# A gated cross-attention and expert layer: the last two chunks turned by row tiles, the upper rows' choice of experts in front of the lower rows, and side work of the first slots moved

## The chip, the cores and the metric

The kernel runs on one core of a Trainium2 chip. The metric is the device time of one execution in microseconds, lower is better. The core's engines each work through a queue of their own in order: TensorE (PE: matmuls; PEld: its weight loads), VectorE (DVE), ScalarE (ACT), GpSimd (POOL), and SyncE (SP), which here only issues transfers. They wait for one another through semaphores.

## The reference

The input `x` has 8 batches of 512 rows and 2048 columns, in float32. First a windowed cross-attention is added to it, then a mixture of expert biases:

```python
def _layernorm(x, axis=-1, eps=1e-05): ...
# attention, in windows of 128 columns; 8 heads of 32; W* are 256 x 512, Wo is 512 x 256
q = Wq @ patches(layernorm(x)) + bq;  k = Wk @ patches(layernorm(x)) + bk;  v = Wv @ patches(ctx) + bv
attn = softmax(where(mask > 0, q^T k / sqrt(32), -1e9))
o = gelu(attn @ v, exact);  out = (Wo @ o + bo) * mask
x = x + tanh(g_xattn) * out
# experts: each of the 8 x 512 rows (2048 long) chooses 8 of 64
flat = layernorm(x)
scores = softmax(flat @ router_weight^T + router_bias)
topk_w, topk_idx = top_k(scores, 8);  w_dense = topk_w scattered to 64 places
out = flat * topk_w.sum() + w_dense @ expert_bias
x = x + tanh(g_ffn) * out
```

The choice of experts needs a whole row: the row's mean and variance and its 64 logits are sums over all 2048 columns.

## The kernel before

**Tiles.** A batch is cut into four chunks of 512 columns (`NCH = 4`), 32 chunks in all. A chunk is a tile of 128 partitions by four row tiles `m = 0..3` (128 rows each) by 512 columns. Each chunk is two slots `g` of 256 columns, that is of two windows. The main loop runs over the slots `g = 0..61`; the last chunk `z` and what hangs on it is written out behind the loop. The order of all instructions is written by hand (`manual_schedule`): each engine gets its instructions in the order in which the Python code names them, and no planner moves them.

**A slot of the loop.** `scores(g)` makes the heads' scores; `weigh` and `weighed` multiply the weights of slot `g - 2` with the values and copy the result; `maxima` (VectorE) adds the mask and finds each row's maximum, `exps` (ScalarE) takes exponentials and sums, `divide` (a reciprocal on VectorE and a product on GpSimd) normalises, `turn` and `turned` transpose the weights on TensorE and copy them out on ScalarE. `queries_and_keys` makes the queries and keys of the next chunk by a seven-product scheme (L356), whose partial sums go through VectorE (L363 to L383) and GpSimd (L370, L377); the lines L363 and L364, a copy and an add on VectorE, must be done before its fifth block may start. `read_x` takes statistics of later batches (`bn_stats` on VectorE, L245) from pieces called `raw`, and after each piece SP issues the load of the next one. `weight_sums_in_place` (L197) and the scaling of the output bias (L791) run once, ahead of slot 0.

**Behind a chunk.** `gelu` on ScalarE; `attend(ch, m)` multiplies by the output weights (`po`, L524), adds bias and mask on VectorE (L530) and adds the result to the chunk's rows in `xr` on GpSimd or VectorE (L533); `statistics2` takes `bn_stats` of them (L543). `turn_x(ch, k)` transposes 128 columns of all four row tiles (`px`, L548), so it needs all four to be complete. `logits` (`pl`, L559) multiplies the four transposed tiles with the router's weights and `logits_out` (L577) adds them up over the chunks.

**The choice of experts of a batch.** `aggregate` turns statistics into mean and reciprocal deviation (VectorE L228, then seven short GpSimd instructions L230 to L236); `gather` (`pg`, L592) transposes the logits back to rows, `choose` (L622, L625) scales them and takes the maximum, `choose_exps` (ScalarE, L631), `select` (VectorE L646 to L656, GpSimd L657 to L660) finds the top eight and the row's factor and offset, and `turn_weights` (`pw`, L671, and a copy on ScalarE, L675) gives the matrix `wT`. With it part `k = 2 * j + mp` of the batch, chunk `j` and row tiles `2 * mp` and `2 * mp + 1`, is finished: `scale_x` (L687 on GpSimd, L685 on ScalarE) scales the rows, `mixed` (`pb`, L698) multiplies the chosen weights with the experts' biases, and one of three adds the two: `added` on VectorE (L716); `with_x` and `taken_out`, an identity matmul into the same bank (L723) and a copy on ScalarE (L730); or `copied`, a copy on ScalarE and an add on GpSimd (L739, L741). Then `stored` (L707) sends 512 KB to the output, on SP's queue unless another is named.

**The end.** In the last batch `b` the choice is made twice, for the upper row tiles 0 and 1 (`up`) and for the lower ones 2 and 3 (`low`), so that the even parts of the batch may go out while the lower rows are still being made. The chunk `z` is already turned by row tiles (`turn_last`, lines L1105 to L1109), the chunk `z - 1` by columns. Mixed in are the parts 5, 6 and 7 of the batch before. Matmul results behind the loop share six banks in turn (`late`), transposes two banks (`ps_tr`).

Of the kernel before, what the change touches and what calls it, by code (L numbers as in the profile page):

```python
# [9 lines left out]
F32 = mybir.dt.float32  # L10
AF = mybir.ActivationFunctionType
ALU = mybir.AluOpType
# [10 lines left out]
def flamingo_gated_kernel(  # L23
# [170 lines left out]
        nc.vector.tensor_tensor(ws4, w12, ws2, ALU.subtract)  # L194

    def weight_sums_in_place():
        nc.vector.tensor_tensor(w21, w11, w21, ALU.subtract)  # L197
        nc.scalar.activation(w22, w22, AF.Copy, scale=-1.0)

    half = const.tile([P, NM], F32, name="half")  # L200
# [503 lines left out]
    def stored(b, k, queue, i0, i1):  # L704
        j, mp = k // 2, k % 2
        ch, ms = b * NCH + j, slice(2 * mp + i0, 2 * mp + i1)
        queue.dma_start(rows_of(out, b, columns(ch))[:, ms, :], xr[ch][:, ms, :])  # L707
        if ms.stop == NM:
            del xr[ch]
# [25 lines left out]
    def copied(b, k, i):  # L735

        j, mp = k // 2, k % 2
        t = work.tile([P, CW], F32, tag="raw", name=f"mixed_{b}_{k}_{i}", bufs=2)
        nc.scalar.copy(t, held[b, k][i])  # L739
        xc = xr[b * NCH + j][:, 2 * mp + i, :]  # L740
        nc.gpsimd.tensor_tensor(xc, t, xc, ALU.add)  # L741
        if i == 1:
            del held[b, k]
            stored(b, k, nc.sync, 0, 2)

    def mix(b, k):
        mixed(b, k)
        added(b, k)
# [39 lines left out]
    load_later_weights()  # L788

    nc.scalar.activation(tgates, gates, AF.Tanh)  # L790
    nc.vector.tensor_scalar_mul(bo_sb, bo_sb, tgates[:, 0:1])  # L791
    NPIECE = NM * S // SW
    queue = [(b, i) for b in range(1, B) for i in range(NPIECE)]
    for i in range(2):
# [19 lines left out]
    for g in range(NG - NH):  # L814
# [21 lines left out]
        def turn_(k):  # L836
            if g1 is not None:
                turn(g1, k)
                turned(g1, k)
# [24 lines left out]
        def read_x(n, pieces=pieces):  # L864

            for b, i in pieces[:n]:
                stats_x(b, i)
                if queue:
                    load_raw(*queue.pop(0))
            del pieces[:n]  # L870

        exps(g, 0)
        if even:
            if xch is not None:
                for m in (2, 3):
                    attend(xch, m)
                del os_[xch], mks[xch]
            exps(g, 1)
            exps(g, 2)
            if g > 0:  # L880
                mask(nxt)
            read_x(len(over), over)
            turn_(0)
            turn_(1)
            exps(g, 3)
            if fin != 4:
                for k in steps:
                    scale_x(mb, k)
            if g > 0:
                divide(g, 0)  # L890
            if g == 0:
                load_mask(2)
        else:
            exps(g, 1)
            if lch is not None:
                logits(lch)
                logits_out(lch)
            read_x(len(over), over)
            turn_(0)
            exps(g, 2)  # L900
            exps(g, 3)
            for k in steps:
                scale_x(mb, k)
            if g > 1:
                divide(g, 0)
            b1 = g // SPB + 1
            if g % SPB == 5 and b1 < B:
                ln1[b1] = aggregate(st1.pop(b1), S // 512, f"1_{b1}")
                shares_of_mean(b1)


        def between(i):
            if even:
                if g == 0 and i == 0:
                    divide(g, 0)
                    mask(nxt)
                turn_x_(i)
            elif i == 0:
                if g == 1:
                    divide(g, 0)  # L920
                turn_(1)
                if fin == 3:
                    gather_halves(b4)
                if pch is not None:
                    gelu(pch)
            else:
                turn_(2)
                if pch is not None and nxt < last:
                    load_mask(nxt + 1)
# [19 lines left out]
        def stats():  # L949

            sch = xch if fin != 4 else None
            if fin == 5:
                sch = ch - 2
            if sch is not None:
                for m in range(NM):
                    statistics2(sch, m)
            read_x(PER)

        if fin != 4:
            stats()  # L960
# [120 lines left out]
    mix(b - 1, 4)  # L1081

    late += [0, 1, 2, 3, None, None]
    for m in (0, 1):
        attend(z - 1, m, tag=t_raw)
    turn_(g, 2, 3)
    for m in range(NM):
# [2 lines left out]
    weigh(g)  # L1090
    weighed(g)
    gelu(z)

    table_of_exps()
    attend(z - 1, 3, tag=t_raw)
    scale_x(b - 1, 5)
    for m in (0, 1):
        statistics2(z - 1, m)


    xz = work.tile([P, KC, NM, P], F32, tag="xn", name="xz")
    for k in range(KC):
        x1T[z, k] = xz[:, k, :, :]

    def turn_last(m):  # L1105
        px = ps_tr.tile([P, KC, P], F32, tag="tr", name=f"px_{z}_m{m}")
        for k in range(KC):
            nc.tensor.transpose(px[:, k, :], xr[z][:, m, k * P : (k + 1) * P], ident)
        nc.scalar.copy(xz[:, :, m, :], px)  # L1109

    def rows_known(ms):
        nmean, rs = aggregate(st2[b], NCH, f"2_{b}", ms[0], ms[-1] + 1)
        experts.setdefault(b, {}).update(nmean=nmean, rs=rs)

    up, low = range(NM // 2), range(NM // 2, NM)
    attend(z, 0, engine=nc.vector, tag=t_raw)
    statistics2(z, 0)
    turn_x(z - 1, 0)
    attend(z, 1, engine=nc.vector, tag=t_raw)
    statistics2(z, 1)  # L1120
    rows_known(up)
    scale_x(b - 1, 6)
    turn_x(z - 1, 1)
    mixed(b - 1, 5)
    for k in range(2, KC):
        turn_x(z - 1, k)
    for m in low:
        statistics2(z - 1, m)
    added(b - 1, 5)
    turn_last(0)  # L1130
    turn_last(1)
    logits(z - 1)
    logits_out(z - 1)
    logits(z, slice(0, NM // 2))
    logits_out(z, slice(0, NM // 2))
    mixed(b - 1, 6, stop=False)
    gather(b, up)
    choose(b, up)
    choose_exps(b, up)
    scale_x(b - 1, 7)  # L1140
    attend(z, 2, engine=nc.vector, tag=t_raw)
    statistics2(z, 2)
    with_x(b - 1, 6, 0)
    taken_out(b - 1, 6, 0)
    attend(z, 3, engine=nc.vector, tag=t_raw)
    statistics2(z, 3)
    rows_known(low)
    select(b, up)
    turn_last(2)
    with_x(b - 1, 6, 1)  # L1150
    taken_out(b - 1, 6, 1)
    turn_last(3)
    mixed(b - 1, 7)
    logits(z, slice(NM // 2, NM))
    logits_out(z, slice(NM // 2, NM))
    turn_weights(b, (0,))
    gather(b, low)
    choose(b, low)
    choose_exps(b, low)
    added(b - 1, 7)  # L1160

    scale_x(b, 0)
    scale_x(b, 2, range(2), nc.scalar)
    scale_x(b, 4)
    mixed(b, 0, stop=False)
    for i in range(2):
        with_x(b, 0, i)
        taken_out(b, 0, i)
    mixed(b, 2)
    select(b, low)  # L1170
    turn_weights(b, (1,))
    added(b, 2)
    scale_x(b, 6, range(2), nc.scalar)
    mix(b, 4)
    scale_x(b, 1)
# [5 lines left out]
    for i in range(2):  # L1181
        copied(b, 3, i)
        scale_x(b, 7, (i,), nc.scalar)
    mix(b, 5)
    mixed(b, 7)
    added(b, 7, (nc.sync, nc.scalar))
# [33 lines left out]
```

## Time and profile before

| | |
|---|---|
| median of three runs | 1313.66 us (1313.34 to 1313.7) |
| the profiled execution | 1313.84 us |
| its span in the profile | 1311.7 us |
| TensorE busy | 1294.1 us, 99% |
| VectorE, ScalarE, GpSimd busy | 923.1, 875.6 and 795.4 us |
| moved by transfers | 173.40 MB, mean 132 GB/s |

The span is the time from the first to the last event of the profile; the execution's own time has about 2.1 us more around it. A busy TensorE is one with a matmul in flight. In rows of the timeline the first number is the start in us from the span's start, the second the duration, and a bracket at the end gives the idle time of that engine just before the row and what ended it. In the chain of waits TensorE has 92% of the span; VectorE has 3%, ScalarE 2%.

### The profile page before, as it was taken

The numbers are of one execution on the slowest core, as the hardware profiler recorded it, in microseconds if no ns is written. First come the engines' busy times: TensorE is split into PE (matmuls) and PEld (weight loads), VectorE is DVE, ScalarE is ACT, GpSimd is POOL, SyncE is SP. The second block draws the span as 40 slices with busy tenths as digits, with TensorE's granted clock in tenths as the row PEclk, the third lists the DMA queues.
The fourth block names the chain that finished last, engine by engine and source line by source line (L and its number), as shares of the span: only waits on it lengthen the run. The fifth ranks groups of instructions, "written<-read, shape, count | busy, mean of one in ns | idle before, by whom it ended". The sixth has DMA issues, their size and how long they took to land.

```text
span 1311.7 us, 27799 instructions
## 1 busy us (share of the span) xinstructions
PE 1294.1 (99%) x9544; PEld 944.4 (72%) x9544; DVE 923.1 (70%) x3607; ACT 875.6 (67%) x2843; POOL 795.4 (61%) x815
## 2 busy tenths in 40 slices
PE   8999999999999999999999999999999999999997
PEld 6777777777777777777777777777777777777653
DVE  4777667677677767777677776677776776666776
ACT  2776776676675776856676766677756767657654
POOL 3655556775566755576655666656666665566644
PEclk9999999999999999999999999999999999999999
DMA  8344424253344452454443453433544413423224
GB/s 288 95 122 112 112 92 137 99 168 112 131 153 150 134 168 92 138 168 134 148 138 105 153 169 122 161 106 125 165 150 132 161 62 125 138 100 101 74 73 176
DMA packets 109693, 173.40 MB, mean 132 GB/s; under 512 B 9200, under 2 KB 43632, under 8 KB 109424
## 3 DMA queue, kind: packets, MB, share of 16 engines
q1 hardware_dynamic: 107776, 169.27, 40.0%
q10 hardware_dynamic: 1776, 2.36, 0.5%
q8 instruction: 75, 1.23, 0.4%
q14 instruction: 66, 0.54, 0.2%
HBM read 138.06 MB, written 33.55 MB: 131 GB/s over the span
## 4 chain that ended last, share of the span: by engine, by line
PE 92%; DVE 3%; ACT 2%; DMA 1%; issue 0%; POOL 0%; SPq 0%; DVEq 0%; ACTq 0%
PE qk L356 27%; PE po L524 17%; PE pv L393 15%; PE pt L472 8%; PE sc L418 5%; PE pa L494 5%; PE pb L698 5%; PE pl L559 4%; PE px L548 4%; ACT at L449 1%; PE pf L323 1%; DVE st L543 1%; DMA cx<-in_ctx 1%; DVE at L437 0%; DVE st L245 0%
## 5 line engine op out<-in xcount | busy, mean ns | idle before, releaser
L458 POOL TENSOR_TENSOR at<-at,rsum 128x1024 f32<-128x1024 f32 x128 | 244.1, 1907 | 291.4 <-DVE rsum L457 274.3
L449 ACT ACTIVATE at<-at,nmx 128x128 f32<-128x128 f32 x1024 | 399.1, 396 | 3.0 <-DVE nmx L437 3.0
L393 PE MATMUL pv<-wv_sb,cx 128*128 128x256 f32 x1024 | 238.5, 381 | 2.4 <-DMA cx<-in_ctx 2.4
L524 PE MATMUL po<-o,wo_sb 128*128 128x512 f32 x512 | 234.1, 599 | 0.4 <-ACT o L518 0.4
L437 DVE CUSTOM_DVE_ANT_0 at<-sc,m 128x128 f32<-128x128 f32 x1024 | 220.8, 287 | 7.8 <-PE sc L418 7.8
L393 PEld LDWEIGHTS pv<-wv_sb,cx 128*128 128x128 f32 x1024 | 188.4, 191 | 25.0 <-DMA cx<-in_ctx 2.8
L533 POOL TENSOR_TENSOR xr<-t,xr 128x512 f32<-128x512 f32 x124 | 161.4, 1314 | 65.9 <-DVE t L530 65.9
L449 ACT ACTIVATION_READ_ACCUMULATOR at<-at,nmx 128x1 f32 x1024 | 198.8, 194 | 0.0
L476 ACT COPY o<-pa 128x512 f32<-128x512 f32 x63 | 37.0, 587 | 229.0 <-PE pa L494 229.0
L476 ACT COPY atT<-pt 128x512 f32<-128x512 f32 x254 | 141.2, 579 | 52.8 <-PE pt L472 52.6
L524 PEld LDWEIGHTS po<-o,wo_sb 128*128 128x128 f32 x512 | 94.3, 190 | 100.6 <-issue 83.9
L472 PEld LDWEIGHTS pt<-ident,at 128*128 128x128 f32 x1024 | 121.7, 141 | 56.7 <-issue 35.3
L472 PE MATMUL pt<-ident,at 128*128 128x128 f32 x1024 | 150.6, 275 | 0.7 <-ACT atT L476 0.3
L530 DVE SCALAR_TENSOR_TENSOR t<-po,bo_sb,mk 128x512 f32<-128x512 f32 x128 | 95.9, 749 | 62.9 <-PE po L524 62.9
L476 ACT COPY x1T<-px 128x512 f32<-128x512 f32 x120 | 70.4, 587 | 95.6 <-PE px L548 95.5
L356 PE MATMUL qk<-xt,wq_sb 128*128 128x256 f32 x496 | 128.0, 381 | 2.0 <-DVE u L364 2.0
L356 PE MATMUL qk<-xn,wk_sb 128*128 128x256 f32 x496 | 127.5, 380 | 0.0
L356 PE MATMUL qk<-xn,ws 128*128 128x256 f32 x496 | 127.3, 379 | 0.0
L356 PEld LDWEIGHTS qk<-xn,ws 128*128 128x128 f32 x496 | 94.2, 190 | 12.8
L716 DVE TENSOR_TENSOR xr<-pb,xr 128x512 f32<-128x512 f32 x122 | 78.2, 686 | 29.4 <-PE pb L698 29.4
L356 PEld LDWEIGHTS qk<-xn,wk_sb 128*128 128x128 f32 x496 | 89.4, 190 | 9.7
L418 PEld LDWEIGHTS sc<-ks,qs 32*128 32x128 f32 x2048 | 63.2, 186 | 45.3 <-DVE t L530 18.2
(123 smaller groups left out, 2081.9 us busy)
## 6 DMA issues: line engine op xcount, KB each, us to landing
out_dram<-xr SPq DMA_DIRECT2D x63, 512.0 KB, 3.5
cx<-in_ctx SPq DMA_DIRECT2D x62, 512.0 KB, 5.3
raw<-in_x SPq DMA_DIRECT2D x112, 256.0 KB, 3.4
xn<-in_x SPq DMA_DIRECT2D x28, 1024.0 KB, 7.7
xr<-in_x SPq DMA_DIRECT2D x28, 1024.0 KB, 7.6
mk<-in_mask_Bx1x_ff SPq DMA_DIRECT2D x32, 256.0 KB, 5.1
xr<-in_x SPq DMA_DIRECT2D x12, 256.0 KB, 6.3
cx<-in_ctx ACTq DMA_DIRECT2D x2, 512.0 KB, 6.5
```

The source lines that it names most:

```text
L356: nc.tensor.matmul(out_, w_[:, j, es], xb[:, j, :], start=(j == 0), stop=(j == NM // 2 - 1))
L393: nc.tensor.matmul(pv[:, i, :], cx[:, m, i * W : (i + 1) * W], wv_sb[:, m, :], start=(m == 0), stop=(m == NM - 1),)
L418: nc.tensor.matmul(sc[r][:, i, e, :], qss[ch][rows[r], e, ws], kss[ch][rows[r], e, ws], start=True, stop=True,)
L437: nc.vector.tensor_tensor_reduce(p["at"][i][:, e * HR + r, :], p["sc"][r][:, i, e, :], bias, -1.0, BIG, ALU.add, ALU.min, p["nmx"][:, r, i ...
L449: nc.scalar.activation(at, at, AF.Exp, bias=p["nmx"][:, r, i, e : e + 1], scale=-1.0, accum_out=p["rsum"][:, i, h : h + 1],)
L458: (engine or nc.gpsimd).tensor_tensor(p["at"][i], p["at"][i], rs[:, :, None].to_broadcast([P, H, W]), ALU.mult)
L472: nc.tensor.transpose(pt[:, r, :], p["at"][i][:, e * HR + r, :], ident)
L476: (engine.tensor_copy if engine is nc.vector else engine.copy)(out_, in_)
L524: nc.tensor.matmul(po[:, cs], wo_sb[:, e, m * P : (m + 1) * P], os_[ch][:, e, cs], start=(e == 0), stop=(e == NE - 1),)
L530: nc.vector.scalar_tensor_tensor(t[:, cs], po[:, cs], bo_sb[:, m : m + 1], mks[ch][:, cs], ALU.add, ALU.mult)
L533: (engine or nc.gpsimd).tensor_tensor(xc, t[:, cs], xc, ALU.add)
L716: nc.vector.tensor_tensor(xc, pt, xc, ALU.add)
```

## The change

In the first slots, the subtract of `weight_sums_in_place` and the scaling of `bo_sb` go from VectorE to GpSimd. `read_x` is left out at the end of slot 0, and slot 1 takes those two pieces in the middle of `queries_and_keys` instead of behind the logits.

At the end, both chunks `z - 1` and `z` are turned by row tiles (`turn_row`). In front stands what the choice of the upper rows needs: the upper rows of both chunks, their logits, `gather`, `choose` and `choose_exps`. The lower rows of `z - 1` and `z` follow, with `select` and `turn_weights` of the upper rows among them, and the lower rows' choice is made among the first finished parts of the last batch. The store of part 3 is named behind that of part 5.

```diff
@@ -194,7 +194,7 @@
         nc.vector.tensor_tensor(ws4, w12, ws2, ALU.subtract)
 
     def weight_sums_in_place():
-        nc.vector.tensor_tensor(w21, w11, w21, ALU.subtract)
+        nc.gpsimd.tensor_tensor(w21, w11, w21, ALU.subtract)
         nc.scalar.activation(w22, w22, AF.Copy, scale=-1.0)
 
     half = const.tile([P, NM], F32, name="half")
@@ -741,7 +741,6 @@
         nc.gpsimd.tensor_tensor(xc, t, xc, ALU.add)
         if i == 1:
             del held[b, k]
-            stored(b, k, nc.sync, 0, 2)
 
     def mix(b, k):
         mixed(b, k)
@@ -788,7 +787,7 @@
     load_later_weights()
 
     nc.scalar.activation(tgates, gates, AF.Tanh)
-    nc.vector.tensor_scalar_mul(bo_sb, bo_sb, tgates[:, 0:1])
+    nc.gpsimd.tensor_scalar_mul(bo_sb, bo_sb, tgates[:, 0:1])
     NPIECE = NM * S // SW
     queue = [(b, i) for b in range(1, B) for i in range(NPIECE)]
     for i in range(2):
@@ -895,7 +894,8 @@
             if lch is not None:
                 logits(lch)
                 logits_out(lch)
-            read_x(len(over), over)
+            if g > 1:
+                read_x(len(over), over)
             turn_(0)
             exps(g, 2)
             exps(g, 3)
@@ -924,6 +924,8 @@
                 if pch is not None:
                     gelu(pch)
             else:
+                if g == 1:
+                    read_x(len(over), over)
                 turn_(2)
                 if pch is not None and nxt < last:
                     load_mask(nxt + 1)
@@ -954,7 +956,9 @@
             if sch is not None:
                 for m in range(NM):
                     statistics2(sch, m)
-            read_x(PER)
+
+            if g > 0:
+                read_x(PER)
 
         if fin != 4:
             stats()
@@ -1081,7 +1085,30 @@
     mix(b - 1, 4)
 
     late += [0, 1, 2, 3, None, None]
-    for m in (0, 1):
+
+
+    up, low = range(NM // 2), range(NM // 2, NM)
+    rows_ = {}
+    for ch in (z - 1, z):
+        rows_[ch] = rows = work.tile([P, KC, NM, P], F32, tag="xn", name=f"rows_{ch}")
+        for k in range(KC):
+            x1T[ch, k] = rows[:, k, :, :]
+
+    def turn_row(ch, m):
+        px = ps_tr.tile([P, KC, P], F32, tag="tr", name=f"px_{ch}_m{m}")
+        for k in range(KC):
+            nc.tensor.transpose(px[:, k, :], xr[ch][:, m, k * P : (k + 1) * P], ident)
+        nc.scalar.copy(rows_[ch][:, :, m, :], px)
+
+    def rows_known(ms):
+        nmean, rs = aggregate(st2[b], NCH, f"2_{b}", ms[0], ms[-1] + 1)
+        experts.setdefault(b, {}).update(nmean=nmean, rs=rs)
+
+    def last_rows(m):
+        attend(z, m, engine=nc.vector, tag=t_raw)
+        statistics2(z, m)
+
+    for m in up:
         attend(z - 1, m, tag=t_raw)
     turn_(g, 2, 3)
     for m in range(NM):
@@ -1090,86 +1117,67 @@
     weigh(g)
     weighed(g)
     gelu(z)
-
     table_of_exps()
-    attend(z - 1, 3, tag=t_raw)
+    for m in up:
+        statistics2(z - 1, m)
     scale_x(b - 1, 5)
-    for m in (0, 1):
-        statistics2(z - 1, m)
-
-
-    xz = work.tile([P, KC, NM, P], F32, tag="xn", name="xz")
-    for k in range(KC):
-        x1T[z, k] = xz[:, k, :, :]
-
-    def turn_last(m):
-        px = ps_tr.tile([P, KC, P], F32, tag="tr", name=f"px_{z}_m{m}")
-        for k in range(KC):
-            nc.tensor.transpose(px[:, k, :], xr[z][:, m, k * P : (k + 1) * P], ident)
-        nc.scalar.copy(xz[:, :, m, :], px)
-
-    def rows_known(ms):
-        nmean, rs = aggregate(st2[b], NCH, f"2_{b}", ms[0], ms[-1] + 1)
-        experts.setdefault(b, {}).update(nmean=nmean, rs=rs)
-
-    up, low = range(NM // 2), range(NM // 2, NM)
-    attend(z, 0, engine=nc.vector, tag=t_raw)
-    statistics2(z, 0)
-    turn_x(z - 1, 0)
-    attend(z, 1, engine=nc.vector, tag=t_raw)
-    statistics2(z, 1)
+    for m in up:
+        turn_row(z - 1, m)
+    for m in up:
+        last_rows(m)
     rows_known(up)
     scale_x(b - 1, 6)
-    turn_x(z - 1, 1)
+    ups, lows = slice(0, NM // 2), slice(NM // 2, NM)
+    logits(z - 1, ups)
+    logits_out(z - 1, ups)
+    for m in up:
+        turn_row(z, m)
+    attend(z - 1, 3, tag=t_raw)
+    logits(z, ups)
+    logits_out(z, ups)
     mixed(b - 1, 5)
-    for k in range(2, KC):
-        turn_x(z - 1, k)
-    for m in low:
-        statistics2(z - 1, m)
-    added(b - 1, 5)
-    turn_last(0)
-    turn_last(1)
-    logits(z - 1)
-    logits_out(z - 1)
-    logits(z, slice(0, NM // 2))
-    logits_out(z, slice(0, NM // 2))
-    mixed(b - 1, 6, stop=False)
     gather(b, up)
     choose(b, up)
     choose_exps(b, up)
     scale_x(b - 1, 7)
-    attend(z, 2, engine=nc.vector, tag=t_raw)
-    statistics2(z, 2)
+    added(b - 1, 5)
+    statistics2(z - 1, 2)
+    mixed(b - 1, 6, stop=False)
+    last_rows(2)
     with_x(b - 1, 6, 0)
     taken_out(b - 1, 6, 0)
-    attend(z, 3, engine=nc.vector, tag=t_raw)
-    statistics2(z, 3)
+    select(b, up)
+    scale_x(b, 0)
+    for m in low:
+        turn_row(z - 1, m)
+    turn_weights(b, (0,))
+    statistics2(z - 1, 3)
+    last_rows(3)
     rows_known(low)
-    select(b, up)
-    turn_last(2)
     with_x(b - 1, 6, 1)
     taken_out(b - 1, 6, 1)
-    turn_last(3)
+    logits(z - 1, lows)
+    logits_out(z - 1, lows)
+    turn_row(z, 2)
     mixed(b - 1, 7)
-    logits(z, slice(NM // 2, NM))
-    logits_out(z, slice(NM // 2, NM))
-    turn_weights(b, (0,))
+    turn_row(z, 3)
+    added(b - 1, 7)
+
+    scale_x(b, 2, range(2), nc.scalar)
+    mixed(b, 0, stop=False)
+    logits(z, lows)
+    logits_out(z, lows)
+    with_x(b, 0, 0)
+    taken_out(b, 0, 0)
     gather(b, low)
+    with_x(b, 0, 1)
+    taken_out(b, 0, 1)
+    scale_x(b, 4)
     choose(b, low)
     choose_exps(b, low)
-    added(b - 1, 7)
-
-    scale_x(b, 0)
-    scale_x(b, 2, range(2), nc.scalar)
-    scale_x(b, 4)
-    mixed(b, 0, stop=False)
-    for i in range(2):
-        with_x(b, 0, i)
-        taken_out(b, 0, i)
-    mixed(b, 2)
+    mix(b, 2)
     select(b, low)
     turn_weights(b, (1,))
-    added(b, 2)
     scale_x(b, 6, range(2), nc.scalar)
     mix(b, 4)
     scale_x(b, 1)
@@ -1182,6 +1190,7 @@
         copied(b, 3, i)
         scale_x(b, 7, (i,), nc.scalar)
     mix(b, 5)
+    stored(b, 3, nc.sync, 0, 2)
     mixed(b, 7)
     added(b, 7, (nc.sync, nc.scalar))
 # ---- launch: one core; inputs and outputs as the reference has them ----
```

## The prediction

> **What bounds the kernel now.** I read the page first: its first line of busy times, then the chain.
>
> ```profile
> PE 1294.1 (99%) x9544; PEld 944.4 (72%) x9544; DVE 923.1 (70%) x3607; ACT 875.6 (67%) x2843; POOL 795.4 (61%) x815
> ```
>
> TensorE is busy for all but 17.6 us of the 1311.7 us span, so time can only come from its idle places or from the tail behind its last matmul. The stretches by 25 us show 25.00 of 25 between about 225 and 1225 us; what is idle lies in the first 125 us and in the last 87. The list of who waited for whom gives the early part, TensorE's rows:
>
> ```profile
> PE qk L356 <- DVE u L364: 2.0, 3, 1.1
> ```
>
> Three waits for VectorE in `queries_and_keys`: 0.56 us at 41.1, 1.09 at 50.6, 0.35 at 79.5. The first two are slots 0 and 1. For the end I read each engine's timeline from 1245 us; TensorE's rows first, then VectorE's (start, us, ..., idle before):
>
> ```profile
> 1282.74 0.66 PE L592 MATMUL pg<-ident,lgT 128*128 128x64 f32 x4
> ...
> 1292.00 0.33 PE L671 MATMUL pw<-ident,rest 128*128 128x128 f32 x1
> 1292.57 0.66 PE L592 MATMUL pg<-ident,lgT 128*128 128x64 f32 x4 [0.24 <-DVE lgT L577]
> 1293.16 1.13 PE L698 MATMUL pb<-eb_sb,wT 64*128 64x512 f32 x4
> 1294.89 1.99 PE L723 MATMUL pb<-xr,ident 128*128 128x512 f32 x4 [0.59 <-POOL xr L687]
> 1296.80 1.13 PE L698 MATMUL pb<-eb_sb,wT 64*128 64x512 f32 x4
> 1297.86 0.33 PE L671 MATMUL pw<-ident,rest 128*128 128x128 f32 x1
> 1298.12 6.07 PE L698 MATMUL pb<-eb_sb,wT 64*128 64x512 f32 x24
> ```
>
> ```profile
> 1290.21 0.11 DVE L646 RECIPROCAL es<-es 128x2 f32<-128x2 f32 x1
> ...
> 1291.65 0.29 DVE L656 TENSOR_TENSOR rest<-lg,rest 128x128 f32<-128x128 f32 x1
> ...
> 1298.03 7.38 DVE L716 TENSOR_TENSOR xr<-pb,xr 128x512 f32<-128x512 f32 x12 [0.77 <-PE pb L698]
> ```
>
> `pg` opens a choice of experts, `pw` closes it. For the upper rows 9.3 us lie between, for the lower rows 5.3 us, and TensorE has other matmuls there; neither `pw` makes it wait long. The last add ends at 1305.41. What follows is transfers (stretches: PE, PEld, DVE, ACT, POOL, clock, DMA share, GB/s):
>
> ```profile
> 1302.00:1304.00 2.00, 2.00 (x8) 0.76 (x6) 2.00 (x4) 2.00 (x4) 1.48 (x2) 1.00 1.00 375
> ...
> 1306.00:1308.00 2.00, 0.00 (x0) 0.00 (x0) 0.00 (x0) 0.00 (x0) 0.00 (x0) 0.53 1.02 378
> 1308.00:1310.00 2.00, 0.00 (x0) 0.00 (x0) 0.00 (x0) 0.00 (x0) 0.00 (x0) 0.50 1.03 383
> 1310.00:1312.00 2.00, 0.00 (x0) 0.00 (x0) 0.00 (x0) 0.00 (x0) 0.00 (x0) 0.50 0.06 21
> ```
>
> The last batch stores 8 x 512 KB. At 380 GB/s that is 1.38 us each, 11.0 in all; they run from 1298.4 to 1310.1 almost without a gap. So the end is set by when stores can start and by holes between them, and only then by the last add.
>
> **The start.** Leaving VectorE ahead of slot 0's `maxima`: the subtract of L197 (0.60 from start to start) and the product of L791 (0.13), less 0.1 for the mask bias to land: `maxima` starts at 36.17, not 36.79, and with it L363 and L364, so the wait of 0.56 at 41.1 goes, 0.6 us. On GpSimd the two cost 1.27 (row L282, same shape) and 0.29 (row L658); its queue is free from 35.76 to 41.85, and the subtract's reader, the fifth block of L356, comes at 40.5. Nothing.
> Two `bn_stats` leave slot 0 (45.20 to 46.35, 1.15 us), so slot 1's `maxima` can start 1.75 earlier and the wait of 1.09 goes too. But ScalarE is late next: behind the exponentials of slot 0 it runs four norms (2.92 us), starts slot 1's exponentials at 45.65 in place of 46.66, and the fourth transpose of slot 0's weights needs its copy: at 52.9, not 53.96. So 1.05 us stay of 1.7. The `bn_stats` reappear between L378 and L382, where VectorE idles 0.43: `qs` then comes 0.2 late with 3 us to its reader. SP takes the `cx` load past two `raw` loads; those are issued about 7 us later and land near 55 to 56 (3.5 us each), where VectorE waits about 1 us for them, ahead of `vT` at 57.1: cover is 0.9 us. After this TensorE is full, so I carry **-1.05** to the end; bounds -0.4 (slow landing) and -1.7 (no wait for ScalarE).
>
> **The end.** I laid every instruction from 1265.6 us on end to end in each engine's order, with the rows' durations: `po` 1.78 a pair, four transposes 0.45, half `pl` 0.92, `pb` 0.53, `L723` 0.86, mask-and-bias 0.75, add 0.70, `bn_stats` 0.62, copy 0.49, GpSimd add 1.27, scale 0.76, statistics chain 2.3, selection 1.75 to `rest`, restart after a wait 0.12. Laid so, the order of before gives its last add at 1305.1 (trace 1305.4) and TensorE waits of 2.1 us. The new order:
> 1. `po` of the last chunk waits for `gelu`: ScalarE ends it at 1270.3. Before, `po` of row 3 (1.78) covered that; now only two `turn_row` (0.9): wait 1.1. Second `turn_row(z,1)` waits 0.8 for VectorE's add.
> 2. `pg` of the upper rows starts at 1280.5, not 1282.4: 1.9 earlier, since 2.8 us of lower-row work is behind it.
> 3. Next come `pb` 6, `po(z,2)` (ends 1284.0), L723, two `turn_row`, done at 1285.6, then `pw`. But on VectorE the selection is queued behind `po(z,2)`'s three instructions (t, add, stats: 1284.0 to 1286.2), and ends at 1288.0. Wait **2.5**, and everything behind `pw` is held: `po(z,3)`, the lower logits.
> 4. So the lower rows' `pg` slips from 1292.3 to 1296.8. Behind it only L723 (0.86) and `pb` 2 (1.06) stand before the lower `pw`; the chain is `choose` and maximum 0.85, exponentials at 1298.8 (behind the second `taken_out` on ScalarE), two adds of part 2 (to 1300.1), selection to 1301.9. Wait **2.8**.
> TensorE waits 7.1 against 2.1; fewer restarts give back 0.3: its last matmul and the last add come 4.6 us later, at 1309.8. GpSimd's add of row 3 of `z-1` goes behind the statistics chain and a scale, ending at 1282.3 with its reader at 1285.1: free. Its scale of part 4 goes behind the lower rows' statistics chain, ending at 1296.8 for an add at 1303: free. On SP the stores of the batch before shift by +3.3, +2.5 and -0.6 us; none of their buffers is wanted again. Stores: part 0 is issued at 1298.9 (1297.2), part 2 at 1300.2, but part 4 only at 1304.4 (1299.7): a hole of 2.7 us in the transfers. Six stores remain, 8.3 us from 1305.7: last transfer ends 1314.0 against 1310.2. Part 3's store behind part 5's lets part 5 out without waiting for GpSimd; in before that wait cost one 0.3 us hole. The end: **+3.8**; bounds +2.7 (the shortest landing, 2.7 us, after the last issue) and +4.6.
>
> **The clock, row against rule.** The trace has one earlier long wait of TensorE:
>
> ```profile
> 12.30 8.86 PE L393 MATMUL pv<-wv_sb,cx 128*128 128x256 f32 x32 [2.36 <-DMA cx<-in_ctx]
> ```
>
> ```profile
> 12.50:13.00 0.50, 0.50 (x2) 0.41 (x2) 0.06 (x1) 0.00 (x0) 0.34 (x2) 0.50 1.02 358
> ...
> 15.50:16.00 0.50, 0.50 (x3) 0.41 (x2) 0.28 (x2) 0.00 (x0) 0.10 (x1) 0.63 1.12 350
> 16.00:16.50 0.50, 0.50 (x4) 0.42 (x4) 0.00 (x0) 0.00 (x0) 0.42 (x2) 1.00 1.10 348
> ```
>
> After 2.36 us of waiting the granted clock was 0.50 from 12.5 to 15.8: 3.3 us at half speed, 1.7 us lost. After the last matmul (1304.2) it fell at 1306.05, 1.9 us on. Waits of 1.1 us and less left it at 1.00. The Trainium skill, "TensorE: Matmul & The Clock Gate", section "What's actually happening", says the gate closes after a whole idle window of about 3.4 us, in windows that run free of the kernel. By the page neither 2.5 nor 2.8 us closes it, and the sum is -1.05 + 3.8 = +2.75, 1316.4. By the row each can, if it fills over half of a window, which its place decides. An estimate: at 1.9 us filled of 3.4 (3.3 by the row), (3.4 + 2.5 - 2 x 1.9) / 3.4 = 0.6 for the first wait, 0.7 for the second. Each drop costs 1.7 us (0 if it misses; TensorE has no other slack between the two `pw`, and in the last stretch the twelve `pb` set the pace at half clock). I side with the row and count one drop: **+1.7**.
> Sum: -1.05 + 3.8 + 1.7 = +4.45 on the profiled execution's 1313.84 (span 1311.7 and 2.1 around it), which stands 0.18 over the median of 1313.66. From the median: 1318.1.
>
> **Rivals.**
> Both waits close the gate: 1319.8. For: both exceed 2.36. Against: windows may split a wait.
> None does: 1316.4. For: the page. Against: the rows above.
> The start brings nothing, its stalls turning into waits for the late `raw` loads: 1319.1. Against: 0.9 us of cover before `vT`.
> The other side: the earlier upper choice is covered. If VectorE's selection is done when TensorE reaches each `pw`, both waits (5.2 with restarts 5.5) are absent: the last add comes at 1304.3, part 0's store is out at 1296.4, and 8 stores without a hole end 11.0 us after 1297.7, at 1308.7, 1.5 earlier than before; with the start 1311.1, on the edge of 0.2% faster. For: `pg` does come 1.9 earlier. Against: VectorE keeps its order, and the selection stands behind `po(z,2)`. It turns where the two waits together are under 2.5 us.
>
> **How the numbers follow.** One drop 0.38, both 0.28, none 0.16 (by the estimate above, tilted a little to the page), no gain at the start 0.08, covered 0.10. A measurement of this kernel tells about 0.2%, 2.6 us: faster ends at 1311.0, slower begins at 1316.3. "None" lies on the upper limit and "covered" on the lower; half of the one and four tenths of the other fall within. Faster 0.06, same 0.12, slower 0.82. Range 1315.4 to 1320.6: the first four cases, with about 1 us of bounds at either end.
>
> **What would show it.** Right: `pw` L671's two rows with idle of 2 to 3 us before them, released by VectorE's `rest`; lower `pg` at 1295 or later (less the start's 1 us); clock under 1.00 in a stretch after one; a hole in the transfers between parts 2 and 4; the wait of L356 for L364 under 1 us. Wrong: `pw` without idle, or last add before 1307 with the clock at 1.00.

## The result and the profile after

| | before | after |
|---|---|---|
| median | 1313.54 us | 1320.12 us (four runs, 1319.06 to 1320.96) |
| ratio of the times | | 1.0049, 95% interval 1.0038 to 1.0061 |
| the profiled execution | 1313.84 us | 1319.98 us |
| its span | 1311.7 us | 1317.9 us |

The change makes the kernel 6.6 us slower. The prediction said 1318.1 us, with a range of 1315.4 to 1320.6 and 0.82 for slower. The direction and the mechanism are those predicted; the size is near that of its first rival, 1319.8, in which both waits lower the clock.

The page's line of busy times, and TensorE's rows in the list of who waited for whom (us in total, times, longest):

```profile
PE 1294.7 (98%) x9552; PEld 943.3 (72%) x9552; DVE 922.5 (70%) x3606; ACT 872.1 (66%) x2843; POOL 796.3 (60%) x817
```

```profile
PE pw L671 <- DVE rest L656: 5.5, 2, 3.2
...
PE po L524 <- ACT o L518: 1.1, 2, 0.8
...
PE qk L356 <- DVE u L364: 1.0, 2, 0.7
```

The busy times are those of before within a few us. What is new is the first row: TensorE stands still for 5.5 us in two waits for the selection of the experts. The last row is the start: two waits and 1.0 us, where before had three and 2.0.

TensorE's timeline at the end (start, duration, in brackets the idle time before):

```profile
1279.15 0.66 PE L592 MATMUL pg<-ident,lgT 128*128 128x64 f32 x4
...
1286.87 0.30 PE L671 MATMUL pw<-ident,rest 128*128 128x128 f32 x1 [2.36 <-DVE rest L656]
1287.00 3.33 PE L524 MATMUL po<-o,wo_sb 128*128 128x512 f32 x4
...
1297.65 0.55 PE L592 MATMUL pg<-ident,lgT 128*128 128x64 f32 x4
...
1299.05 1.13 PE L698 MATMUL pb<-eb_sb,wT 64*128 64x512 f32 x4
1303.33 0.33 PE L671 MATMUL pw<-ident,rest 128*128 128x128 f32 x1 [3.15 <-DVE rest L656]
1303.59 7.12 PE L698 MATMUL pb<-eb_sb,wT 64*128 64x512 f32 x24
```

The upper rows' `pg` and `pw` come 3.6 and 5.1 us earlier than before, the `pw` after a wait; the lower rows' `pg` and `pw` come 5.1 and 5.5 us later. The four matmuls of `po` behind the first wait (row tile 3) take 3.33 us, where those of row tile 2 took 1.98 at 1280.79; the last 24 `pb` take 7.12 in place of 6.07.

VectorE's timeline shows what the two `pw` wait for:

```profile
1282.82 0.75 DVE L530 SCALAR_TENSOR_TENSOR t<-po,bo_sb,mk 128x512 f32<-128x512 f32 x1 [0.31 <-PE po L524]
1283.60 0.69 DVE L533 TENSOR_TENSOR xr<-t,xr 128x512 f32<-128x512 f32 x1
1284.33 0.69 DVE L543 BATCH_NORM_STATS2 st<-xr 128x6 f32<-128x512 f32 x1
1284.94 0.15 DVE L646 RECIPROCAL es<-es 128x2 f32<-128x2 f32 x1
...
1286.43 0.29 DVE L656 TENSOR_TENSOR rest<-lg,rest 128x128 f32<-128x128 f32 x1
...
1300.28 1.29 DVE L716 TENSOR_TENSOR xr<-pb,xr 128x512 f32<-128x512 f32 x2 [1.17 <-PE pb L698]
1301.49 0.15 DVE L646 RECIPROCAL es<-es 128x2 f32<-128x2 f32 x1
...
1302.98 0.29 DVE L656 TENSOR_TENSOR rest<-lg,rest 128x128 f32<-128x128 f32 x1
```

In each case the selection (L646 to L656, 1.8 us) begins in the very moment in which a group named ahead of it ends: the mask-and-bias, add and statistics of `last_rows(2)` for the upper rows, the two adds of part 2 for the lower rows. The exponentials that it needs had ended on ScalarE at 1281.5 and 1300.4, 3.4 and 1.1 us before. So the upper wait is a matter of VectorE's queue alone. Of the lower wait's 3.15 us the two adds explain 1.1; the rest is the time that the choice itself takes, with too few matmuls named beside it.

The stretches of time (us, busy of PE, PEld, DVE, ACT, POOL, then TensorE's granted clock, DMA share, GB/s) show what the waits do besides:

```profile
1287.00:1288.00 1.00, 1.00 (x3) 0.53 (x3) 0.32 (x1) 0.37 (x1) 0.81 (x3) 0.65 0.00 0
...
1290.00:1291.00 1.00, 1.00 (x3) 0.34 (x1) 0.63 (x1) 0.00 (x0) 0.00 (x0) 0.65 0.00 0
...
1304.00:1305.00 1.00, 1.00 (x6) 0.46 (x4) 0.00 (x0) 1.00 (x3) 0.90 (x3) 0.68 0.00 0
...
1306.00:1307.00 1.00, 1.00 (x4) 0.35 (x2) 0.57 (x2) 0.88 (x2) 1.00 (x2) 0.50 0.00 0
1307.00:1308.00 1.00, 1.00 (x6) 0.38 (x4) 1.00 (x2) 0.00 (x0) 0.13 (x1) 0.62 0.75 287
```

A row of 0.65 is part at 1.00 and part at 0.50, so the steps can be placed: the clock fell at 1287.30 and rose at 1290.70, fell again at 1304.36 and rose at 1307.76. Both waits were followed by 3.4 us at half speed. And the transfers (stretches of 2 us):

```profile
1304.00:1306.00 2.00, 2.00 (x8) 0.89 (x6) 0.97 (x2) 2.00 (x4) 1.90 (x4) 0.59 0.00 0
1306.00:1308.00 2.00, 2.00 (x8) 0.73 (x6) 1.57 (x3) 0.88 (x2) 1.13 (x2) 0.56 0.37 143
...
1314.00:1316.00 2.00, 0.00 (x0) 0.00 (x0) 0.00 (x0) 0.00 (x0) 0.00 (x0) 0.65 1.03 380
```

Between parts 2 and 4 nothing is stored for over 3 us. The next stretch holds only 57 GB/s: the last transfer ends near 1316.3, where before it ended near 1310.1.

### The profile page after: what moved, and what is told of

It is laid out like the page before. It is cut to its first block, busy times and chain, and to the rows that moved or that the text cites. A ratio compares the mean times of both kernels' runs of the same rounds, so it can differ in the third digit from the quotient of the medians.

```text
span 1317.9 us, 27820 instructions
## 1 busy us (share of the span) xinstructions
PE 1294.7 (98%) x9552; PEld 943.3 (72%) x9552; DVE 922.5 (70%) x3606; ACT 872.1 (66%) x2843; POOL 796.3 (60%) x817
## 3 DMA queue, kind: packets, MB, share of 16 engines
q10 hardware_dynamic: 1776, 2.36, 0.5%
## 4 chain that ended last, share of the span: by engine, by line
PE 92%; ACT 3%; DVE 3%; DMA 1%; issue 0%; SPq 0%; DVEq 0%; ACTq 0%
PE qk L356 27%; PE po L524 17%; PE pv L393 15%; PE pt L472 8%; PE sc L418 5%; PE pb L698 5%; PE pa L494 5%; PE pl L559 4%; PE px L548 4%; ACT at L449 2%; PE pf L323 1%; DVE st L543 1%; DMA cx<-in_ctx 1%; DMA xr<-in_x 1%; ACT atT L476 0%
## 5 line engine op out<-in xcount | busy, mean ns | idle before, releaser
L449 ACT ACTIVATION_READ_ACCUMULATOR at<-at,nmx 128x1 f32 x1024 | 195.1, 191 | 0.0
L476 ACT COPY atT<-pt 128x512 f32<-128x512 f32 x254 | 140.6, 576 | 52.9 <-PE pt L472 52.7
```

What stands on the lines that cost most here:

```text
L449: nc.scalar.activation(at, at, AF.Exp, bias=p["nmx"][:, r, i, e : e + 1], scale=-1.0, accum_out=p["rsum"][:, i, h : h + 1],)
L476: (engine.tensor_copy if engine is nc.vector else engine.copy)(out_, in_)
```

## The experiments

### Which half of the change costs

`start_only` is before with the edits of the first slots alone, `end_only` is before with the new order of the end alone.

```diff
@@ weight_sums_in_place
-        nc.vector.tensor_tensor(w21, w11, w21, ALU.subtract)
+        nc.gpsimd.tensor_tensor(w21, w11, w21, ALU.subtract)
-    nc.vector.tensor_scalar_mul(bo_sb, bo_sb, tgates[:, 0:1])
+    nc.gpsimd.tensor_scalar_mul(bo_sb, bo_sb, tgates[:, 0:1])
@@ slots 0 and 1
-            read_x(len(over), over)
+            if g > 1:
+                read_x(len(over), over)
...
+                if g == 1:
+                    read_x(len(over), over)
...
-            read_x(PER)
+            if g > 0:
+                read_x(PER)
```

> The kernel before with the three edits of slots 0 and 1 alone, its end unchanged. My theory (the start gains 1.05 us, since ScalarE's copy takes the rest of 1.7 back): 1312.5 us. Rival (the gain in the trace after is mostly the first 20 us, where the clock did not drop this time, and only half of it is the edits): 1313.0. Rival (nothing stays): 1313.5.

> The kernel before with the new order of the end alone, start unchanged. My theory: +3.8 us from the order and 1.7 for each of the two drops of the clock, 1319.0 with one and 1320.7 with both. Rival (the order alone, the clock costs nothing): 1317.3.

Measured: `start_only` 1312.24 us, ratio 0.9991 (0.9983 to 0.9999); ten of its thirteen runs lie at 1312.04 to 1312.52 and three at 1313.27 to 1313.43. `end_only` 1320.02 us (1319.42 to 1321.03), ratio 1.0050 (1.0037 to 1.0063). Against the runs of before taken beside them (1313.63) the end alone loses 6.4 us and the start alone wins 1.4. The medians of after and `end_only` lie too close to show that gain again, since their runs spread over 1.9 and 1.6 us. Their profiles show it: in `end_only` the two `pw` start at 1287.77 and 1304.22, in after at 1286.87 and 1303.33, 0.90 and 0.89 us earlier.

### The upper rows' wait taken away

`select_first` is after with the selection of the upper rows named ahead of `last_rows(2)`. No work is left out.

```diff
     mixed(b - 1, 6, stop=False)
+    select(b, up)
     last_rows(2)
     with_x(b - 1, 6, 0)
     taken_out(b - 1, 6, 0)
-    select(b, up)
```

> The changed kernel with the upper rows' selection on VectorE ahead of the three instructions of row tile 2 of the last chunk, not behind them. Theory (the selection stands behind po of that row tile, and this makes the upper transpose L671 wait): that wait of 2.4 us goes and with it one drop of the clock: 2.3 + 1.7 less, 1316.1. If the drop costs nothing: 1317.8. Rival (the selection is late for another reason, its exponentials or the gather): the wait stays, 1320.1.

Measured: 1317.61 us (1316.79 to 1318.36), ratio 1.0030 (1.0018 to 1.0041), 2.5 us under after. Its TensorE rows, and its clock:

```profile
1284.45 0.30 PE L671 MATMUL pw<-ident,rest 128*128 128x128 f32 x1
...
1299.21 0.47 PE L671 MATMUL pw<-ident,rest 128*128 128x128 f32 x1 [3.15 <-DVE rest L656]
1299.61 7.95 PE L698 MATMUL pb<-eb_sb,wT 64*128 64x512 f32 x24
```

```profile
1298.00:1299.00 1.00, 0.00 (x0) 0.00 (x0) 0.93 (x8) 0.00 (x0) 0.31 (x2) 0.50 0.63 240
...
1304.00:1305.00 1.00, 1.00 (x6) 0.52 (x4) 0.79 (x2) 0.00 (x0) 0.00 (x0) 0.63 0.99 381
```

The first `pw` has no idle time before it: the wait was for the place of the selection on VectorE, and for nothing else. The second is untouched, 3.15 us, and here the clock stays at half for 6.8 us, from 1297.96 to 1304.75, so that the 24 `pb` take 7.95 us. One would count 4.1 us for the wait (2.36 and a drop of 1.7). The profiled execution, 1316.81 us, is 3.2 under after's: from the lower `pw` to the end of the last add it takes 10.08 us where after takes 9.10, so the longer drop took the other 1.0 back. The median's 2.5 has the spread of the start in it as well, and what the executions without a profile did is not shown.

### The clock by itself: the waits filled with matmuls

`filled` is after with matmuls of ones, read by nothing, put in front of the two `pw`: 16 for the upper and 20 for the lower rows. If the drop of the clock is what the waits cost beyond their length, they should take it away.

```diff
+    def filler(n, name):
+        px = ps_tr.tile([P, P], F32, tag="tr", name=name)
+        for _ in range(n):
+            nc.tensor.matmul(px, ones, ones, start=True, stop=True)
...
+    filler(16, "fill_u")
     turn_weights(b, (0,))
...
+    filler(20, "fill_l")
     turn_weights(b, (1,))
```

> The changed kernel with matmuls of ones into an unread bank ahead of the two transposes L671 of the weights: 16 ahead of the upper, 20 ahead of the lower, 0.11 us each, so that TensorE works through most of each wait. Nothing else starts sooner or later by order. Theory (waits of 2.4 and 3.2 us close the clock gate, and each closing costs 1.7 us): the two transposes stand where they stood after the upper wait, the clock stays at 1.00, and the time falls by 3.4 us, to 1316.7. Rival (the waits alone carry the loss, the clock in the records costs nothing): 1320.1, or more if the added matmuls delay the transposes.

Measured: 1321.47 us (1319.77 to 1322.37), ratio 1.0059 (1.0046 to 1.0072).

```profile
1284.69 3.84 PE L1114 MATMUL fill_u<-ones 128*128 128x128 f32 x32 [0.29 <-ACT rows L1101]
```

As a test of the clock this failed on its size. A transpose of 128 x 128 takes 0.11 us in this kernel, and the number was chosen by that; a matmul of ones of the same shape took 0.23. The filling lasted 3.84 us and was longer than the wait: the two `pw` came at 1288.37 and 1304.45, 1.5 and 1.1 us later than in after. All the same the last matmul ended at 1310.73, after's at 1310.71, with the clock at 1.00 throughout. The transfers behind part 2 began later, at 1308.1 against 1307.25, and the kernel was slower by that and a little more. `filled_short` is the same with 7 and 11.

> As filled, but with 7 and 11 matmuls of ones: in filled one took 0.23 us, not 0.11, so that its 16 and 20 outlasted the waits and put the transposes L671 off by 1.5 and 1.6 us. 7 and 11 take 1.6 and 2.6 us of waits of 2.4 and 3.2. Theory (each drop of the clock costs 1.7 us at least): the transposes keep their places, the clock stays at 1.00, 3.4 us less than the changed kernel, 1316.7. Rival (the drops cost nothing): 1320.1.

Measured: 1318.19 us (two runs at 1317.17 and 1317.28, three at 1318.19 to 1318.44), ratio 1.0033 (1.0021 to 1.0046).

```profile
1285.99 1.83 PE L1114 MATMUL fill_u<-ones 128*128 128x128 f32 x14 [0.29 <-ACT rows L1101]
1287.97 0.33 PE L671 MATMUL pw<-ident,rest 128*128 128x128 f32 x1
...
1299.55 2.72 PE L1114 MATMUL fill_l<-ones 128*128 128x128 f32 x22
1302.77 0.33 PE L671 MATMUL pw<-ident,rest 128*128 128x128 f32 x1 [0.50 <-DVE rest L656]
1303.03 6.07 PE L698 MATMUL pb<-eb_sb,wT 64*128 64x512 f32 x24
```

Now the filling ends with the wait, and the useful work stands as late as in after: from the transposes ahead of it (1284.67 here, 1283.47 in after) to the upper `pw` it is 3.30 us against 3.40. The clock stays at 1.00. From the upper `pw` to the lower one it is 14.80 us in place of 16.46, and from the lower `pw` to the end of the last add 7.54 in place of 9.10. Those two differences, 1.66 and 1.56 us, are the price of the two drops at the last add. At the last transfer less of it is left: `filled_short`'s ends near 1314.8 and after's near 1316.3, and since `filled_short` came to the upper `pw`'s transposes 1.2 us later, the drops are worth about 2.7 us of the kernel's time. In its slower three runs, the profiled one among them, something was lost at the start, which is the subject of the experiments further below; the two others lie 2.9 us under after's median.

### Both waits covered

`both_covered` is `select_first` with the lower rows' `gather`, `choose` and exponentials one step earlier, and their selection ahead of the adds of part 2, with the matmuls of parts 2 and 4 in front of `turn_weights`.

```diff
+    gather(b, low)
     with_x(b, 0, 0)
     taken_out(b, 0, 0)
-    gather(b, low)
     with_x(b, 0, 1)
-    taken_out(b, 0, 1)
-    scale_x(b, 4)
     choose(b, low)
     choose_exps(b, low)
-    mix(b, 2)
+    taken_out(b, 0, 1)
+    scale_x(b, 4)
+    mixed(b, 2)
+    mixed(b, 4)
     select(b, low)
     turn_weights(b, (1,))
     scale_x(b, 6, range(2), nc.scalar)
-    mix(b, 4)
+    added(b, 2)
+    added(b, 4)
```

> The changed kernel with the upper selection ahead of row tile 2 on VectorE, and for the lower rows the gather one matmul group earlier, the choice's exponentials ahead of the second taken_out on ScalarE, the selection ahead of the adds of part 2 on VectorE, and part 4's matmuls ahead of the lower transpose L671. Both waits are then covered by order. Theory (waits and their clock drops make the loss): by the same laying out of instructions the last transfer ends 2.9 us earlier than in the changed kernel without drops, and no drop is left: 1320.1 - 3.4 - 2.9 = 1313.8, level with before. Rival (turning by row tiles costs something else at the end, a transfer or a bank): 1316 or more.

Measured: 1313.60 us (thirteen runs, 1313.21 to 1314.50), ratio 1.0001 (0.9993 to 1.0009).

```profile
1285.55 0.30 PE L671 MATMUL pw<-ident,rest 128*128 128x128 f32 x1
...
1299.12 0.30 PE L671 MATMUL pw<-ident,rest 128*128 128x128 f32 x1 [0.49 <-DVE rest L656]
1299.35 5.59 PE L698 MATMUL pb<-eb_sb,wT 64*128 64x512 f32 x20
```

The same end, with VectorE's queue in another order, gives back all of the loss. It is not better than before: it stands 1.4 us above `start_only`, which has the same start and the old end. This is the prediction's rival of the other side carried out. Its price of 1311.1 was too low by 2.5 us. That rival let eight stores follow one another without a hole; here the adds of parts 2 and 4 wait for the selection, and the transfers stand still for a microsecond behind part 0's store:

```profile
1299.00:1300.00 1.00, 0.88 (x4) 0.71 (x5) 1.00 (x2) 0.55 (x2) 0.72 (x4) 1.00 0.91 346
1300.00:1301.00 1.00, 1.00 (x7) 0.48 (x4) 1.00 (x3) 1.00 (x2) 1.00 (x2) 1.00 0.00 0
```

### The start: which edit, and why two groups

The runs of `start_only`, `filled_short` and `both_covered`, which have the new start, fall in two groups about 1 us apart; those of before do not. The next kernels asked what that is, and what each edit is worth. `weights_only` moves L197 and L791 and leaves `read_x` in place; `start_store` is `start_only` with the store of part 3 behind that of part 5.

```diff
@@ copied
-            stored(b, k, nc.sync, 0, 2)
@@ the end
     mix(b, 5)
+    stored(b, 3, nc.sync, 0, 2)
     mixed(b, 7)
```

> The kernel before with the subtract L197 and the product L791 on GpSimd alone; reads of x as before. start_only took 1.4 us. Theory (the first wait of 0.56 us goes by these two, ScalarE's and VectorE's later queue keep it): 0.6 less, 1313.0. Rival (the gain of start_only is all from the moved reads): 1313.6.

> start_only with the store of part 3 named behind that of part 5, as in the changed kernel; the order of the end otherwise as before. Theory (part 5's store need not wait for GpSimd's add, and the hole of 0.3 us in the last transfers closes): 0.3 us less than start_only, 1311.9. Rival (the transfers of the tail are one queue and order in it makes no difference): 1312.2.

Measured: `weights_only` 1312.77 us (nine runs at 1312.50 to 1313.00, four at 1313.80 to 1314.04), ratio 0.9996 (0.9988 to 1.0004); `start_store` 1312.50 us (seven at 1312.02 to 1312.50, six at 1313.02 to 1313.37), ratio 0.9993 (0.9985 to 1.0001). In the lower group the two moved instructions are worth about 0.8 us and the moved `bn_stats` 0.5 more; the order of the stores is worth nothing that can be seen (1312.1 against 1312.2 in the lower group, 1313.2 against 1313.4 in the upper). In the upper group `weights_only` is slower than before.

The profiles tell the groups apart. VectorE's mask bias L299 and GpSimd's L197 in after, whose early clock stayed at 1.00:

```profile
35.18 0.93 DVE L299 TENSOR_SCALAR m<-m 128x512 f32<-128x512 f32 x1
36.26 0.29 DVE L437 CUSTOM_DVE_ANT_0 at<-sc,m 128x128 f32<-128x128 f32 x1 [0.15 <-PE sc L418]
```

```profile
34.56 1.27 POOL L287 TENSOR_TENSOR xt<-xt,xn 128x512 f32<-128x512 f32 x1
35.79 1.45 POOL L197 TENSOR_TENSOR wq_sb<-wk_sb,wq_sb 128x512 f32<-128x512 f32 x1
```

And in the profile of `start_only`, an execution of the upper group (1313.4 us), with its clock:

```profile
35.76 1.56 DVE L299 TENSOR_SCALAR m<-m 128x512 f32<-128x512 f32 x1
37.48 0.29 DVE L437 CUSTOM_DVE_ANT_0 at<-sc,m 128x128 f32<-128x128 f32 x1 [0.15 <-DVE m L299]
```

```profile
35.77 1.27 POOL L197 TENSOR_TENSOR wq_sb<-wk_sb,wq_sb 128x512 f32<-128x512 f32 x1
```

```profile
15.00:16.00 1.00, 1.00 (x4) 0.78 (x3) 0.87 (x3) 0.40 (x1) 0.01 (x1) 0.50 1.10 348
```

In TensorE's early wait for `cx` the clock drops or not, from one execution to the next. Here are the waits of `start_only`, where it dropped, and of after, where it did not:

```profile
12.35 8.86 PE L393 MATMUL pv<-wv_sb,cx 128*128 128x256 f32 x32 [2.12 <-DMA cx<-in_ctx]
```

```profile
12.36 3.72 PE L393 MATMUL pv<-wv_sb,cx 128*128 128x256 f32 x16 [2.51 <-DMA cx<-in_ctx]
```

The longer wait is the one without a drop. The clock changes on a grid of 3.413 us (last section), and what differs is the place on it: `start_only`'s wait, 10.23 to 12.35, lies whole in the window that ends with the drop at 13.29; after's grid, counted back from the drop at 1287.30, cuts the wait there at 10.71, into 0.86 and 1.65 us. If it drops, everything is 0.6 us later at 35 us, and L299 starts together with L197 on GpSimd and does not end until L197 has, 0.3 us after it: 1.56 us, and the maxima start at 37.48 in place of 36.26. If it does not drop, L299 starts while L287 still runs, ends 0.3 us after L287, and L197 is the one that is stretched (1.45 us). In before L197 stands on VectorE behind L299, and nothing on GpSimd follows L287, which ends at 35.76: L299 ends at about 36.1 whether the clock drops (this row) or not (36.06 in `before_warm` below).

```profile
35.72 0.43 DVE L299 TENSOR_SCALAR m<-m 128x512 f32<-128x512 f32 x1
```

The profiles of `start_only`, `weights_only`, `filled_short` and `both_covered` are all of the upper group, and L299 lasts 1.54 to 1.57 us in them; that of `start_store` is of the lower group, and it lasts 1.10. The Trainium skill, "SBUF — State Buffer", section "Who interferes with whom", states the rule behind it: VectorE's `tensor_scalar` can use a pair of ports that it shares with GpSimd, and whichever of the two issues first keeps the pair for its whole instruction. The rows agree with the lock: L299 ends about 0.3 us behind the instruction of GpSimd that it waits for. Which of the two issued first they cannot tell, since L299 and L197 start 0.01 us apart in `start_only`.

Two ways to test it: take the early drop away, or change what stands on GpSimd. `start_warm` and `before_warm` put nine matmuls of ones (2.1 us) into the early wait:

```diff
     for i in range(NPP):
         values(0, 0, i)
+    for _ in range(9):
+        nc.tensor.matmul(warm, ones, ones, start=True, stop=True)
     new_queries_and_keys(0)
```

> start_only with nine matmuls of ones (0.23 us each, 2.1 us) behind the values of the first context tile, in TensorE's early wait for the second one (2.36 us at 9.9 in before). Theory (the two groups of start_only's times, 1312.2 and 1313.4, are executions in which that early wait did not and did drop the clock): the filled wait never drops it, so all runs fall in one group at 1312.1 to 1312.5, the scores of slot 0 begin near 34.2 us, and the clock is 1.00 from 10 to 16 us. Rival (the groups come from something later, such as the landing of a raw piece): two groups remain, about 1.1 us apart, with the scores at 34.2 in both.

> before with the same nine matmuls in the early wait. Theory (the early drop costs what the groups differ by, and before always has it): 1312.4, 1.1 us under before, in one group. Rival 1 (before's start is held by VectorE, so that a full clock in the first 16 us is lost again at the first waits for L364): 1313.5, no change. Rival 2 (the start edits and the clock are worth separate amounts): start_warm lies 0.4 us under before_warm, the amount by which the slow group of start_only lies under before, or 1.3 us under it, if before has no drop in most executions.

Measured: `start_warm` 1312.09 us, eleven runs at 1311.89 to 1312.26, one group, ratio 0.9988 (0.9979 to 0.9997); `before_warm` 1313.60 us (1313.42 to 1313.66), ratio 1.0000 (0.9991 to 1.0008). The upper group is gone from the one, and the other does not move: in before the clock of the first 16 us is worth nothing, its first rival. Its L299 starts at 35.11 and lasts 0.95 us, to the same end as ever.

`start_swap` is `start_only` with the two instructions on GpSimd in the other order, the short one first.

```diff
@@ weight_sums_in_place
-        nc.gpsimd.tensor_tensor(w21, w11, w21, ALU.subtract)
@@ ahead of slot 0
     nc.gpsimd.tensor_scalar_mul(bo_sb, bo_sb, tgates[:, 0:1])
+    nc.gpsimd.tensor_tensor(w21, w11, w21, ALU.subtract)
```

> start_only with the two moved instructions in the other order on GpSimd: the scaling of bo_sb (0.30 to 0.47 us) first, the subtract of L197 (1.27) behind it. Theory (start_only's slow group is the early clock drop, which lets VectorE's L299 begin at 35.76, level with GpSimd's change from L287 to L197, so that L299 lasts till L197 has ended, 1.56 us in place of 0.43): now L299 has only the short instruction ahead of it, or goes between the two, so with the drop maxima begin near 36.5 in place of 37.48 and the slow executions come within 0.3 us of the fast ones: all runs in 1312.0 to 1312.6. Rival (the slow group comes from the dropped clock itself, whatever stands on GpSimd): two groups about 1.1 us apart remain, 1312.2 and 1313.4, with maxima at 36.5 or before in both.

Measured: 1312.33 us, eleven runs at 1312.12 to 1312.82, ratio 0.9991 (0.9982 to 1.0000). No run reaches the upper group (1313.27 and more); of the 52 runs of `start_only`, `both_covered`, `weights_only` and `start_store` 17 are in their upper groups. Two runs, 1312.75 and 1312.82, lie over the band that was expected; they may be the executions with the early drop, but the profiled one had none, so that is not shown. `start_warm` is the fastest version found: 1.5 us, 0.12%, under before.

## Why the prediction was right, point by point

**The upper `pw`.** Predicted: a wait of 2.5 us because the selection is queued behind `po(z,2)`'s three instructions. Measured: 2.36, behind just those three, and gone in `select_first`.

**The lower `pg` and `pw`.** Predicted: `pg` at 1296.8 less the start's 1 us, measured 1297.65, with the first drop's 1.7 us on top; a wait of 2.8 us, measured 3.15. The working let the first add of part 2 start after the first of its two matmul groups, about 1299.7. In the trace the add waited for both, to 1300.18, which is enough for the missing 0.35 us. The rows of before had shown it: its `pb` of part 2 end at 1297.93 and its first add starts at 1298.03.

**The smaller waits.** Predicted 1.1 us for `gelu` and 0.8 for the second `turn_row(z,1)`; measured 0.77 for `po` there and 0.45.

**The clock.** This term was mis-sized. The prediction took the row (2.36 us of waiting, 3.3 us at half speed) over the rule of a whole idle window that it cites from the Trainium skill, and that was right: neither wait fills 3.4 us, and both were followed by a drop. It counted one drop, +1.7, with 0.6 and 0.7 as chances for each; in the profiled execution of after both came. An estimate: with the limit of half a window that all these profiles show (last section) and the waits measured, the same formula gives 0.7 and 0.9, so two drops were the likelier case. Nothing shows that every execution has both: after's four runs, 1319.06 to 1320.96, spread as they would if the drops varied, and the early drop may be in it too.

**The order without the clock.** This term was mis-sized as well. Predicted +3.8. (The working's waits add up to 7.2 us, not 7.1, and leave 4.7, not 4.6; that is rounding.) `filled_short`, whose clock stays at 1.00 at the end, lies 5.0 us over `start_only`, group by group (1317.2 against 1312.2, 1318.4 against 1313.4). Its profile keeps step with before's up to the new order, so the two can be laid side by side: the last add ends at 1310.31, 4.9 us later (predicted 4.6), and the transfers behind the hole begin at about 1306.5, not 1305.7, and end 8.3 us on, as the prediction counted:

```profile
1306.00:1307.00 1.00, 1.00 (x7) 0.59 (x4) 1.00 (x3) 0.56 (x2) 0.57 (x1) 1.00 0.54 207
```

**The end of the transfers.** Predicted with both drops: 6.1 us later than before, with a hole behind part 2. Measured: about 6.2 us later, with that hole. That the sum with two drops, 1319.8, comes so near to 1320.12 is in part luck: the order cost about 1 us more than predicted, and the two drops 2.7 us in place of 3.4.

**The start.** Predicted -1.05, from the wait of 0.56 us that goes, and from ScalarE being late next, at 52.9 us. In after that transpose waits 0.61 us for ScalarE and starts at 52.85:

```profile
40.67 1.10 PE L356 MATMUL qk<-xt,wq_sb 128*128 128x256 f32 x4 [0.67 <-DVE u L364]
```

```profile
52.85 0.66 PE L472 MATMUL pt<-ident,at 128*128 128x128 f32 x4 [0.61 <-ACT atT L476]
```

The gain held, 1.1 us at 53 us; the first wait did not disappear from the rows, since TensorE itself came 0.55 us earlier to it. The step that failed is the word "Nothing" for the two instructions on GpSimd. That engine was free, as the working said, but it is not independent of VectorE: where the clock drops early, L197 holds L299 up for 1.1 us and eats most of the gain: 1313.4 us in `start_only`'s upper group, against 1313.6 in before. The trace from which -1.05 was worked out has that drop (12.5 to 15.8). That after's profiled execution has none, and going by their groups two thirds of the runs with this start, is luck for this term.

**The store of part 3** behind part 5: predicted to close one hole of 0.3 us; `start_store` shows no gain.

## What to carry to other kernels

When a chain is moved forward, look at where its middle stands in the queue of the engine that runs it: here the choice of the upper rows began 3.6 us earlier and waited on VectorE behind three instructions that nobody needed yet. A wait of TensorE of over 2 us must be priced with what it may do to the clock, and a place for a few matmuls in it is worth looking for. And before side work is moved to an idle engine, look at what the other one does in those microseconds: an instruction on an idle GpSimd can still hold up VectorE's `tensor_scalar`.

## What the runs showed of the hardware that was not expected

- The clock changes on a grid: `start_only`'s three changes are recorded 3.413 and 1290.238 us apart, 1 and 378 times 3.413, and after's four 3.413, 13.653 and 3.413, which is 1, 4 and 1 times.
- With the clock at 1.00, a drop came at the end of each such window in which TensorE stood idle for 1.75 us or more, and of none with 1.68 or less, in all thirteen profiles. Both limits are from `start_store`: its tail (last matmul ended at 1302.61, drop at 1304.36) and its early wait, which ends at 12.39, 1.68 us into the window from 10.71. So it took about half a window, not a whole one, and whether a wait of 1.7 to 3.4 us lowers the clock depends on where the grid cuts it: 1.94 us whole in one window did in `both_covered`, 2.58 us cut in two did not in `select_first`.
- One drop can last two windows: 6.8 us in `select_first`, though only the first 1.25 us of the second window was idle. That is too little to lower the clock; in this one case it was too much to raise it.
- A matmul of ones, 128 x 128 in float32, took 0.23 us, a transpose of that shape 0.11.
- VectorE's L299 took 0.43 us in before, with GpSimd at rest from 0.04 us after its start, 0.93 to 1.18 where a GpSimd instruction was running, and 1.56 where one started with it.
